# Layer 0's low half and bias on GpSimd, quarter tiles in layer 3, and a new instruction order: a four-layer graph network on one core

## The chip, the core and the metric

The kernel runs on one core of one Trainium2 chip. The core has five engines, each with its own queue of instructions that it works off in order: TensorE (PE; matrix products, with its weight loads shown as PEld), VectorE (DVE), ScalarE (ACT), GpSimd (POOL) and SyncE (SP, which only starts transfers here). They wait for each other through semaphores. The metric is the time of one execution on the device in microseconds (us); lower is better.

## What is computed

16 graphs of 1024 nodes with 256 features each go through four graph layers. Every layer takes the layer norm of x, cuts it at zero, and adds the layer's result to x.

```python
h = relu(layernorm(x)); x = x + L0(h, adj)   # and so on for L1, L2, L3
# L0: relu(h @ W_upd + (adj^T @ (h @ W_msg)) / deg + bias)
# L1: 4 heads; wh = h @ W; attention = softmax(leaky_relu(e_src[i] + e_dst[j]) where adj)
#     out = relu(attention @ wh + bias) + wh, then a layer norm per head
# L2: 4 heads; the same attention with slope 0.2; elu(attention @ wh)
# L3: 1 head of width 256; attention @ wh
```

The inputs are float32 (adj is int32), and so is the output.

## The kernel before

The kernel has a fast path, `tile_factored`, and a general one behind it (`tile_general`), which runs only when a flag says that the data does not suit the fast one; with these inputs it does not run.

The softmax is factored. The exponent of leaky_relu(s + d) is the larger of two products of a part that depends on the source and one that depends on the target. So for each block of 128 target nodes (`jb`) and each head one VectorE instruction makes a tile of masked weights, `p`: the larger of a row `r` (a source part, spread over all partitions) and a column `tt`, times the mask. It stands in `masked`, line 1083, and works on 128x1024 elements in layers 1 and 2 and on 128x256 in layer 3. PE multiplies p with the projected features and sums over the eight blocks in PSUM (`acc`): 16 products of 64 columns per p in layers 1 and 2 (line 1266, shown as 32 records), two of 257 columns per p in layer 3 (line 1420). The last column of the features is the sum that the result is divided by.

Per graph the stages are:

- `layer0`: norm (`norm_t`: statistics on VectorE at 922 and 929, the inverse root on GpSimd at 934 and 935, normalised rows `hn` on ScalarE at 954, transposes on PE at 967, copies to `ht` at 973); the projection with W_msg (984); the split of the messages into a high half `hi`, rounded to PE's faster float32r, and a low half `lo`. For `lo` PE adds minus `hi` to the projection in PSUM with a product by -I (`minus`, 1119), and ScalarE copies the rest out (1129). Then eight gathers over the adjacency (1143 with hi, 1146 with lo), the degree (1154), its inverse on GpSimd (1157, 1158), the scaled messages `o` (1164); and for each pair of blocks a product of ones with the bias, itself in two float32r halves (`pair`, `b0`, 1173), with the products of h with W_upd on top (1182). VectorE adds `o` and that (1194) and then x (1201).
- `heads` for layers 1 and 2: norm, projection (984, copied out at 1003), `terms`: the source parts are raised (`es`, 1024), turned by PE (1034), copied into a p tile (1038), written to DRAM (`rd`, 1042) and read back spread over the partitions (`r`, 1067); three reductions keep bounds of the exponents for the flag (`f_mx`, 1050 to 1052); the target parts are raised (1057, 1058) and multiplied into the features (`weigh`, 1247). Then 4 heads of 8 p each; after each head an epilogue (`epilogue1`, `epilogue2`; from 1285 on: divide, bias, norm per head with GpSimd's root at 1339 and 1340, or elu with 1381, 1382 and 1388). Three heads are added to x by a DMA that GpSimd starts (1216), the last by VectorE (1227).
- `layer3`: the same with one head; four quarters of the nodes, each with 8 p of 128x256 and two accumulators; then the inverse (1434), the result with x added (1445), and the store (1459).

The order of all this on the engines is not that of the program. Every step is put into a plan by `do`, with its engine, a cost in us, what it reads and writes, and a priority: `plan.pos` (PE work so far, moved by `SHIFT` per graph) plus a number from the table `RANK` for its stage and engine. `Plan.emit` then always issues the step that could start earliest by these costs, the lower priority first among equals. A tile of a kind is there as often as `BUFS` says (six p, two hn, two acc, three x), and a step waits in the plan until one is free. So several graphs are under way at once, and the order on each engine is fixed when the kernel is built. A graph's plan may not begin before layer 3 of the graph two before it (`gates`).

```python
self.ops.append((eng, cost, lag, fn, deps, bufs, self.pos + slack + RANK[self.stage][ENGINES.index(eng)], kind, dma))
...
if at is not None and (best is None or (at, prio, k) < best):
    best = (at, prio, k)
```

Of the kernel before, what the change touches and what calls it, by code (L numbers as in the profile page):

```python
# [8 lines left out]
F32 = mybir.dt.float32  # L9
# [9 lines left out]
P = 128  # L19
# [7 lines left out]
SHIFT = 38.75  # L27

ENGINES = ("pe", "dve", "act", "pool", "sp")
RANK = {  # L30
    "load": (-255, -45, -146, -223, -161),
    "setup": (147, 44, -129, 45, 72),
    "norm0": (132, -159, -111, 18, -3),
    "split0": (-94, 119, -51, -165, -111),
    "mask": (77, 143, 41, 193, 218),
    "gather0": (241, -7, 71, 23, 10),
    "norm1": (-60, -62, -162, -146, -99),
    "project1": (20, 26, -5, 26, -6),
    "weights1": (-164, 7, -45, 57, -13),
    "heads1": (-192, -212, -213, -62, -111),  # L40
    "last1": (-26, -102, 9, -196, -80),
    "norm2": (-206, -157, 81, 6, -21),
    "project2": (79, -60, -360, 87, -40),
    "weights2": (94, -3, 153, -153, 12),
    "heads2": (-112, -33, -288, -105, -59),
    "last2": (-21, -230, -230, -36, -82),
    "norm3": (-477, -373, -518, -355, -261),
    "project3": (148, 162, -14, -78, 0),
    "weights3": (170, 143, 167, 44, 87),
    "last3": (43, -259, -75, -14, -59),  # L50
# [4 lines left out]
    "mv": 4, "st": 2, "rstd": 4, "shift": 4, "tt": 3, "es": 2, "dg": 2, "rden": 2, "sth": 1, "mh": 2, "rsh": 2,  # L55
# [16 lines left out]
class Plan:  # L72
# [8 lines left out]
    def __init__(self):  # L81
        self.ops, self.pos, self.gate, self.stage = [], 0.0, None, None

    def do(self, eng, cost, fn, r=(), w=(), lag=0.0, slack=0.0, kind="f", dma=0.0):
# [25 lines left out]
        self.ops.append((eng, cost, lag, fn, deps, bufs, self.pos + slack + RANK[self.stage][ENGINES.index(eng)], kind, dma))  # L110
# [3 lines left out]
    def emit(self):  # L114
# [7 lines left out]
        kept, moved = "f", 0.0  # L122
# [6 lines left out]
        while ready:  # L129
            best = None  # L130
            for k in ready:
                eng, cost, lag, fn, deps, bufs, prio, kind, dma = self.ops[k]
# [18 lines left out]
                if at is not None and (best is None or (at, prio, k) < best):  # L151
                    best = (at, prio, k)
            at, _, k = best
            eng, cost, lag, fn, deps, bufs, _, kind, dma = self.ops[k]
# [444 lines left out]
def tile_factored(  # L599
# [46 lines left out]
    minus = const.tile([P, P], F32R, name="f_minus")  # L646
    nc.vector.tensor_scalar(minus, ident, -1.0, None, op0=ALU.mult)
# [8 lines left out]
    mx = const.tile([P, B * 9], F32, name="f_mx")  # L656
    rdn = const.tile([P, B * NB], F32, name="f_rdn")

    pair = const.tile([2, 1], F32R, name="f_pair")
    nc.gpsimd.memset(pair.bitcast(F32), 1.0)  # L660
# [24 lines left out]
    b0 = kept("f_bias0", [2, D], F32R)  # L685
# [139 lines left out]
    def weights():  # L825
# [3 lines left out]
        y = buf(work, "y", [P, 2 * D])  # L829
        fetch(y, "in", lambda t: t[0:1, :D], bias0.rearrange("(o d) -> o d", o=1))  # L830

        def parts():
            nc.vector.tensor_copy(b0.t[0:1, :], y.t[0:1, :D])
            nc.vector.tensor_tensor(
                y.t[0:1, D:].bitcast(F32R), y.t[0:1, :D], b0.t[0:1, :].bitcast(F32), op=ALU.subtract
            )

        do("dve", 0.7, parts, r=[(y, "in")], w=[(y, "lo"), (b0, 0)])
        do(
            "pool",  # L840
            0.8,
            lambda: nc.gpsimd.dma_start(b0.t[1:2, :], y.t[0:1, D:].bitcast(F32R)),
            r=[(y, "lo")],
            w=[(b0, 1)],
            lag=2.5,
        )
# [61 lines left out]
    def norm_t(xs, by_block=False):  # L908
# [3 lines left out]
        for hf in range(2):  # L912
# [34 lines left out]
            for i2 in range(2):  # L947
# [21 lines left out]
                do("pe", 0.46, turn, r=[hn], w=[pt])  # L969
# [8 lines left out]
    def project(ps, ht, ib, w, lo, hi, k=0):  # L978


        def go():
            out = ps.t[:, : hi - lo] if hi - lo > D else ps.t[:, k, :]
            for c in range(KC):
                nc.tensor.matmul(  # L984
                    out,
                    ht.t[:, c, ib * P : (ib + 1) * P],
                    w.t[:, c, lo:hi],
                    start=(c == 0 and k == 0),
                    stop=(c == KC - 1),
                    skip_group_check=k > 0,  # L990
                )

        do("pe", 0.88, go, r=[(ht, ib // 2), w], w=[ps])
# [15 lines left out]
    def terms(wh, nh, slope, ecol, scol, k):  # L1009


        tt = buf(small, "tt", [P, NB, nh])
        r4 = buf(work, "p", [P, N])
        rd = buf(dram, "rd", [nh, N])

        def ed():
# [3 lines left out]
        es = buf(small, "es", [P, nh, NB])  # L1020
# [4 lines left out]
                es.t, wh.t[:, :, scol : scol + nh].rearrange("p n h -> p h n"), AF.Exp, scale=1.0 - slope  # L1025
            ),
            r=[(wh, ib) for ib in range(NB)],
            w=[es],
# [5 lines left out]
            lambda: nc.tensor.transpose(pt.t[:m, :P], es.t.rearrange("p h n -> p (h n)"), ident),  # L1034
            r=[es],
# [12 lines left out]
        def bounds():  # L1048
            es = wh.t[:, :, scol : scol + nh]
            nc.vector.tensor_reduce(mx[:, k : k + 1], ed(), AX.XY, ALU.max)  # L1050
            nc.vector.tensor_reduce(mx[:, k + 1 : k + 2], ed(), AX.XY, ALU.min, negate=True)
            nc.vector.tensor_reduce(mx[:, k + 2 : k + 3], es, AX.XY, ALU.max)

        do("dve", 0.4, bounds, r=[wh])

        def raise_t():
            nc.scalar.activation(tt.t, ed(), AF.Exp, scale=-(1.0 - slope))
            nc.scalar.activation(ed(), ed(), AF.Exp)

        do("act", 0.5, raise_t, w=[tt, wh])  # L1060
# [14 lines left out]
        return tt, spread  # L1075

    def masked(r, tt, mask, jb, h, lo, hi):

        w = buf(work, "p", [P, N])
# [4 lines left out]
                w.t[:, : hi - lo], r.t[:, lo:hi], tt.t[:, jb, h : h + 1], mask.t[:, jb, lo:hi], op0=ALU.max, op1=ALU.mult  # L1084
            ),
            r=[r, tt, mask],
            w=[w],
# [4 lines left out]
    def layer0(b, xs, adjr, mask):  # L1092
# [11 lines left out]
        for n in range(0, NB, 2):  # L1104
            ps = buf(mm_p, "mm", [P, 2, D])
            for k in range(2):
# [9 lines left out]
            do(  # L1116
                "pe",
                0.23,
                lambda n=n, ps=ps: nc.tensor.matmul(
                    ps.t, minus, hi.t[:, n : n + 2, :D], start=False, stop=True, skip_group_check=True  # L1120
                ),
                r=[(hi, ib) for ib in parts],
                w=[ps],
                kind="r",
            )
# [3 lines left out]
                lambda n=n, ps=ps: nc.scalar.copy(lo.t[:, n : n + 2, :D], ps.t),  # L1129
                r=[ps],  # L1130
                w=[(lo, ib) for ib in parts],
# [4 lines left out]
        for jb in range(NB):  # L1136
# [35 lines left out]
            def update(pu=pu, j0=jb - 1):  # L1172
                nc.tensor.matmul(
                    pu.t,
                    pair.to_broadcast([2, P]),
                    b0.t.rearrange("k (o d) -> k o d", o=1).to_broadcast([2, 2, D]),
                    start=True,
                    stop=False,
                )
                for q in range(2):  # L1180
                    for c in range(KC):
# [4 lines left out]
                            start=False,  # L1186
                            stop=(q == 1 and c == KC - 1),
                        )

            do("pe", 2.17, update, r=[(ht, jb // 2), (dg, "in"), w0, b0], w=[pu], kind="rf")  # L1190
# [42 lines left out]
    def heads(b, l, xs, mask, w, slope, epilogue, keep):  # L1233
# [19 lines left out]
        for h in range(H):  # L1253
# [5 lines left out]
            for jb in range(NB):  # L1259
# [14 lines left out]
                do("pe", 0.94, product, r=[p, xw], w=[ps], kind="c")  # L1274
# [276 lines left out]
```

## Time and profile before

| | before |
|---|---|
| median of 3 runs | 2740.81 us (2739.89 to 2741.58) |
| the profiled execution | 2741.27 us, span 2739.4 us |
| PE's granted clock, mean over the span | 0.972 of full |
| masked weights, 128x1024 (L1083, VectorE) | 1024 instructions, 1251.0 us busy, mean 1276 ns |
| masked weights, 128x256 (L1083, VectorE) | 512 instructions, 222.4 us busy, mean 477 ns |
| head products (L1266, PE) | 32768 records, 1064.6 us busy; 135.7 us idle before them |
| layer 3 products (L1420, PE) | 2048 records, 462.2 us busy; 10.1 us idle before them |
| GpSimd's inverse root of the heads (L1340) | 64 instructions of 128x8, mean 2348 ns |
| row r read back (L1067, SyncE's queue) | 144 transfers, median 3.9 us from issue to landing |

The profile is of one execution, and its span is what lies between the first and the last instruction. A group of instructions is given by line, engine, operation, tiles (out<-in) and shapes, with its busy time and mean duration; behind the bar stands how long the engine was idle just before such instructions, and what ended that. Instructions of one engine overlap a little, so that busy times count a bit double: p of 128x1024 takes 1276 ns, but the next one starts 1196 ns after it. In a timeline every line has a start, a duration, the engine and the instruction, merged where several of one kind follow each other; a bracket shows the idle time before it and who ended it.

### The profile page before, as it was taken

The page shows a single profiled execution, that of the slowest core. Times are in us where ns is not written, and L with a number is a line of the kernel's source. Part 1 is how long each engine was busy: PE and PEld are TensorE (multiplying, and loading weights), DVE is VectorE, ACT ScalarE, POOL GpSimd, SP SyncE. Part 2 cuts the span into 40 slices and gives each one's busy share as a digit, 9 for nine tenths or more (in the row PEclk, how much of TensorE's full clock was granted, in tenths as well). Part 3 has the DMA queues.
Part 4 walks back from the last instruction along what each step waited for, and adds up shares of the span by engine and source line. Part 5 has one row for each costly group of instructions (what it writes and reads, how often), then busy time and mean ns, then how long its engine had stood idle before and what let it go on. Part 6 is the DMA issues. An engine that isn't in the chain of part 4 may idle for free. (4 is left out here: it accounts for less than half of the span.)

```text
span 2739.4 us, 92386 instructions
## 1 busy us (share of the span) xinstructions
PE 2547.4 (93%) x40667; PEld 2285.7 (83%) x40667; DVE 2357.3 (86%) x4790; ACT 1143.5 (42%) x2753; POOL 878.0 (32%) x907
## 2 busy tenths in 40 slices
PE   7867999999999999999999999999999999999786
PEld 6767798888888888889888889888888988888775
DVE  2699689898988989899898989989898898989884
ACT  4431625344353444525344452534435353453222
POOL 3332234324252332424224251422425133241210
PEclk9989999999999999999999999999999999999998
DMA  8724547356472745547255563735546263562121
GB/s 194 171 44 84 113 87 165 82 128 117 99 143 53 159 91 129 105 91 163 60 144 97 118 125 71 163 75 133 112 107 134 63 158 81 130 118 66 33 52 29
DMA packets 397318, 293.58 MB, mean 107 GB/s; under 512 B 179301, under 2 KB 345706, under 8 KB 396906
## 3 DMA queue, kind: packets, MB, share of 16 engines
q0 software_dynamic: 232992, 92.29, 24.8%
q1 hardware_dynamic: 160752, 193.05, 24.4%
q8 instruction: 321, 5.26, 0.8%
q10 hardware_dynamic: 3162, 2.24, 0.3%
q14 instruction: 91, 0.75, 0.1%
HBM read 228.21 MB, written 17.37 MB: 90 GB/s over the span
## 5 line engine op out<-in xcount | busy, mean ns | idle before, releaser
L1083 DVE SCALAR_TENSOR_TENSOR p<-r,tt,mask 128x1024 f32<-128x1024 f32 (+1 forms) x1536 | 1473.3, 1010 | 109.2 <-PE acc L1266 40.8
L1266 PE MATMUL acc<-wide,p 128*64 128x65 f32 x32768 | 1064.6, 227 | 135.7 <-DVE p L1083 129.3
L1266 PEld LDWEIGHTS acc<-wide,p 128*64 128x64 f32 x32768 | 1017.2, 141 | 204.0 <-issue 99.0
L984 PE MATMUL mm<-f_w,ht 128*128 128x264 f32 (+2 forms) x2048 | 477.0, 387 | 1.4 <-ACT ht L973 1.3
L1420 PE MATMUL acc<-wide,p 128*128 128x257 f32 x2048 | 462.2, 382 | 10.1 <-DVE p L1083 9.9
L1420 PEld LDWEIGHTS acc<-wide,p 128*128 128x128 f32 x2048 | 386.1, 191 | 68.1 <-issue 11.1
L984 PEld LDWEIGHTS mm<-f_w,ht 128*128 128x128 f32 x2048 | 384.6, 192 | 61.2 <-ACT ht L973 3.0
L954 ACT ACTIVATE hn<-x,shift,rstd 128x256 f32<-128x256 f32 x512 | 269.1, 591 | 257.5 <-DVE shift L941 157.1
L1356 ACT ACTIVATE t<-t,mh,rsh 128x64 f32<-128x64 f32 x512 | 176.7, 428 | 198.2 <-DVE mh L1346 174.3
L1143 PE MATMUL mm<-wide,adjr 128*128 128x258 f32 x1024 | 254.5, 289 | 0.0
L1146 PE MATMUL mm<-wide,adjr 128*128 128x256 f32 x1024 | 247.9, 282 | 0.0
L1003 ACT COPY wide<-mm 128x264 f32<-128x264 f32 (+1 forms) x384 | 141.3, 378 | 218.7 <-PE mm L984 216.5
L1216 POOL DMA_DIRECT2D x<-y x48 | 76.6, 1596 | 447.4 <-DVE y L1388 435.8
L934 POOL TENSOR_SCALAR rstd<-mv 128x4 f32<-128x4 f32 x128 | 60.7, 474 | 434.6 <-DVE mv L929 402.3
L1143 PEld LDWEIGHTS mm<-wide,adjr 128*128 128x128 f32 x1024 | 195.9, 191 | 1.7
L1146 PEld LDWEIGHTS mm<-wide,adjr 128*128 128x128 f32 x1024 | 194.2, 190 | 1.5
L922 DVE BATCH_NORM_STATS2 st<-x 128x6 f32<-128x256 f32 x512 | 183.2, 412 | 8.4 <-DMA x<-in_x_dram 5.6
L967 PE MATMUL mm<-f_ident,hn 128*128 128x128 f32 x1024 | 168.0, 300 | 20.2 <-ACT hn L954 17.2
L973 ACT COPY ht<-mm 128x512 f32<-128x512 f32 x256 | 137.8, 580 | 104.9 <-PE mm L967 103.9
L1157 POOL TENSOR_SCALAR dg<-f_deg 128x1 f32<-128x1 f32 x128 | 61.0, 476 | 359.7 <-ACT f_deg L1154 357.4
L967 PEld LDWEIGHTS mm<-f_ident,hn 128*128 128x128 f32 x1024 | 125.2, 151 | 50.4 <-ACT hn L954 35.5
L935 POOL TENSOR_TENSOR rstd<-rstd,f_mhalf 128x4 f32<-128x4 f32 x128 | 162.2, 1268 | 10.7
(103 smaller groups left out, 2179.3 us busy)
## 6 DMA issues: line engine op xcount, KB each, us to landing
r<-rd SPq DMA_DIRECT2D x144, 512.0 KB, 3.9
adjr<-in_adj_dram POOLq DMA_DIRECT2D x128, 512.0 KB, 4.7
nat<-in_adj_dram SPq DMA_DIRECT2D x128, 512.0 KB, 6.6
out_dram<-o SPq DMA_DIRECT2D x64, 256.0 KB, 2.8
x<-in_x_dram SPq DMA_DIRECT2D x31, 512.0 KB, 5.1
x<-t POOLq DMA_DIRECT2D x48, 256.0 KB, 5.5
x<-y POOLq DMA_DIRECT2D x48, 256.0 KB, 4.5
mask<-sq SPq DMA_TRANSPOSE x128, 4.7
```

Source lines behind the costliest of these rows:

```text
L922: lambda st=st, ib=ib, k=k: nc.vector.bn_stats(st.t[:, k, :], xs.t[:, ib, :]),
L935: nc.gpsimd.tensor_tensor(rstd.t, rstd.t, mhalf[:, :nh], op=ALU.pow)
L954: nc.scalar.activation(hn.t[:, k, :], xs.t[:, hf * nh + q, :], AF.Relu, bias=shift.t[:, q : q + 1], scale=rstd.t[:, q : q + 1],)
L967: nc.tensor.transpose(pt.t[:, k, c, :], hn.t[:, k, c * P : (c + 1) * P], ident)
L984: nc.tensor.matmul(out, ht.t[:, c, ib * P : (ib + 1) * P], w.t[:, c, lo:hi], start=(c == 0 and k == 0), stop=(c == KC - 1), skip_group_che ...
L1003: lambda ib=ib, ps=ps: nc.scalar.copy(wh.t[:, ib, :cols], ps.t[:, :cols]),
L1083: lambda: nc.vector.scalar_tensor_tensor(w.t[:, : hi - lo], r.t[:, lo:hi], tt.t[:, jb, h : h + 1], mask.t[:, jb, lo:hi], op0=ALU.max, op1= ...
L1143: nc.tensor.matmul(ps.t[:, : D + 2], a.t[:, ib, :], hi.t[:, ib, : D + 2], start=(ib == 0), stop=False)
L1146: nc.tensor.matmul(ps.t[:, :D], a.t[:, ib, :], lo.t[:, ib, :D], start=False, stop=(ib == NB - 1))
L1266: nc.tensor.matmul(ps.t[c : c + 64, g, q * E1 : (q + 1) * E1], p.t[:, i2 * 64 : (i2 + 1) * 64], xw.t[:, jb, h * E1 : (h + 1) * E1], start= ...
L1356: nc.scalar.activation(t.t[:, ib, :], t.t[:, ib, :], AF.Identity, bias=mb.t[:, 3, ib : ib + 1], scale=rs.t[:, ib : ib + 1],)
L1420: nc.tensor.matmul(ps.t[:, q, : D + 1], w.t[:, q * P : (q + 1) * P], wh.t[:, jb, : D + 1], start=(jb == 0), stop=(jb == NB - 1),)
```

## The change

The parts of the diff are these.

- Layer 0's low half: the product by -I is gone. ScalarE copies the whole projection from PSUM into a tile of the kind hn (`raw`), and GpSimd subtracts hi from it, 128x512 elements at a time, four times a graph.
- Layer 0's bias: the product with ones is gone, with `pair` and the split of the bias. The bias is loaded once, spread over all partitions, and GpSimd adds it to the scaled messages `o`, 128x512 at a time, four times a graph.
- Layer 3: four p of 128x256 share one p tile, a quarter each, so that six tiles hold 24.
- `terms`: the raised source and target parts lie in one tile `et`, the turned source part has a tile of its own (`r4`) instead of a p tile, and the bounds are taken after raising with two reductions instead of three, with a later priority.
- The plan: a new `RANK` and `SHIFT`, a starting number for each graph (`START`), p kept in the order of the program within a graph (`row`), p put first when none is in stock (`LOW`, `FIRST`), a hold that lets a step of lower priority number go first if it could start a little later (`HOLD`), and some costs changed. The order on every engine comes out differently.

```diff
-SHIFT = 38.75
+SHIFT = 50.0
+
+LOW, FIRST = 1, 288
 
 ENGINES = ("pe", "dve", "act", "pool", "sp")
+HOLD = (0.0, 0.25, 0.05, 0.0, 0.0)
+
+START = (428, 493, 356, 309, 254, 248, 242, 107, 64, 31, -43, -148, -235, -329, -280, -568)
 RANK = {
...
-    "gather0": (241, -7, 71, 23, 10),
+    "gather0": (-34, -156, -171, 38, -118),
...
-    "weights1": (-164, 7, -45, 57, -13),
+    "weights1": (-176, 10, 31, -19, 1),
...
-    "mv": 4, "st": 2, "rstd": 4, "shift": 4, "tt": 3, "es": 2, "dg": 2, "rden": 2, "sth": 1, "mh": 2, "rsh": 2,
+    "mv": 4, "st": 2, "rstd": 4, "shift": 4, "et": 3, "r4": 1, "dg": 2, "rden": 2, "sth": 1, "mh": 2, "rsh": 2,
...
+        if row is not None:
+            if row in self.rows:
+                deps.add(self.rows[row])
+            self.rows[row] = k
+        self.ops.append((eng, cost, lag, fn, deps, bufs, self.pos + slack + RANK[self.stage][ENGINES.index(eng)], kind, dma, stock))
...
+                if stock > 0 and store < LOW:
+                    prio -= FIRST
...
-                if at is not None and (best is None or (at, prio, k) < best):
-                    best = (at, prio, k)
-            at, _, k = best
-            eng, cost, lag, fn, deps, bufs, _, kind, dma = self.ops[k]
+                if at is not None:
+                    could.append((at, prio, k))
+                    if best is None or could[-1] < best:
+                        best = could[-1]
+            at, prio, k = best
+            until = at + HOLD[ENGINES.index(self.ops[k][0])]
+            for a, p, q in could:
+                if self.ops[q][0] == self.ops[k][0] and a <= until and p < prio:
+                    at, prio, k = a, p, q
+            eng, cost, lag, fn, deps, bufs, _, kind, dma, stock = self.ops[k]
+            store += stock
...
-    b0 = kept("f_bias0", [2, D], F32R)
+    b0 = kept("f_bias0", [P, D])
...
+        fetch(b0, "in", lambda t: t, bias0.rearrange("(o d) -> o d", o=1).to_broadcast([P, D]))
...
+        def raise_t():
+            nc.scalar.activation(et.t[:, 1], ed().rearrange("p n h -> p h n"), AF.Exp, scale=-(1.0 - slope))
+            nc.scalar.activation(ed(), ed(), AF.Exp)
+
+        do("act", 0.5, raise_t, w=[(et, 1), wh])
+
         def bounds():
-            es = wh.t[:, :, scol : scol + nh]
-            nc.vector.tensor_reduce(mx[:, k : k + 1], ed(), AX.XY, ALU.max)
-            nc.vector.tensor_reduce(mx[:, k + 1 : k + 2], ed(), AX.XY, ALU.min, negate=True)
-            nc.vector.tensor_reduce(mx[:, k + 2 : k + 3], es, AX.XY, ALU.max)
-
-        do("dve", 0.4, bounds, r=[wh])
-
-        def raise_t():
-            nc.scalar.activation(tt.t, ed(), AF.Exp, scale=-(1.0 - slope))
-            nc.scalar.activation(ed(), ed(), AF.Exp)
-
-        do("act", 0.5, raise_t, w=[tt, wh])
+            nc.vector.tensor_reduce(mx[:, k : k + 2], et.t.rearrange("p s h n -> p s (h n)"), AX.X, ALU.max)
+            nc.vector.tensor_reduce(mx[:, k + 2 : k + 3], ed(), AX.XY, ALU.max)
+
+        do("dve", 0.45, bounds, r=[et, wh], slack=24.857)
...
+    def masked(r, tt, mask, jb, h, lo, hi, w=None, q=0):
+
+
+        w = w or buf(work, "p", [P, N])
+        c = q * (hi - lo)
         do(
             "dve",
             (hi - lo + 125) / 960.0,
             lambda: nc.vector.scalar_tensor_tensor(
-                w.t[:, : hi - lo], r.t[:, lo:hi], tt.t[:, jb, h : h + 1], mask.t[:, jb, lo:hi], op0=ALU.max, op1=ALU.mult
+                w.t[:, c : c + hi - lo],
+                r.t[:, lo:hi],
+                tt.t[:, 1, h, jb : jb + 1],
+                mask.t[:, jb, lo:hi],
+                op0=ALU.max,
+                op1=ALU.mult,
             ),
-            r=[r, tt, mask],
-            w=[w],
+            r=[r, (tt, 1), mask],
+            w=[(w, q)],
+            row="weights",
+            stock=1,
...
-            do(
-                "pe",
-                0.23,
-                lambda n=n, ps=ps: nc.tensor.matmul(
-                    ps.t, minus, hi.t[:, n : n + 2, :D], start=False, stop=True, skip_group_check=True
-                ),
-                r=[(hi, ib) for ib in parts],
-                w=[ps],
-                kind="r",
-            )
+            raw = buf(work, "hn", [P, 2, D])
             do(
                 "act",
                 0.48,
-                lambda n=n, ps=ps: nc.scalar.copy(lo.t[:, n : n + 2, :D], ps.t),
+                lambda raw=raw, ps=ps: nc.scalar.copy(raw.t, ps.t),
                 r=[ps],
+                w=[raw],
+            )
+            do(
+                "pool",
+                1.3,
+                lambda n=n, raw=raw: nc.gpsimd.tensor_tensor(
+                    lo.t[:, n : n + 2, :D],
+                    raw.t,
+                    hi.t[:, n : n + 2, :D].bitcast(F32),
+                    op=ALU.subtract,
+                ),
+                r=[raw, *((hi, ib) for ib in parts)],
                 w=[(lo, ib) for ib in parts],
...
             def update(pu=pu, j0=jb - 1):
-                nc.tensor.matmul(
-                    pu.t,
-                    pair.to_broadcast([2, P]),
-                    b0.t.rearrange("k (o d) -> k o d", o=1).to_broadcast([2, 2, D]),
-                    start=True,
-                    stop=False,
-                )
                 for q in range(2):
                     for c in range(KC):
                         nc.tensor.matmul(
                             pu.t[:, q, :],
                             ht.t[:, c, (j0 + q) * P : (j0 + q + 1) * P],
                             w0.t[:, c, D:],
-                            start=False,
-                            stop=(q == 1 and c == KC - 1),
+                            start=(q == 0 and c == 0),
+                            stop=(c == KC - 1),
+                            skip_group_check=q > 0,
                         )
 
-            do("pe", 2.17, update, r=[(ht, jb // 2), (dg, "in"), w0, b0], w=[pu], kind="rf")
+            do("pe", 1.78, update, r=[(ht, jb // 2), (dg, "in"), w0], w=[pu])
+            do(
+                "pool",
+                1.3,
+                lambda o=o: nc.gpsimd.tensor_tensor(
+                    o.t, o.t, b0.t.rearrange("p (o d) -> p o d", o=1).to_broadcast([P, 2, D]), op=ALU.add
+                ),
+                r=[b0],
+                w=[o],
+            )
...
-                w = masked(r, tt, mask, jb, 0, i2 * 2 * P, (i2 + 1) * 2 * P)
-
-                def product(w=w, ps=ps, jb=jb):
-                    for q in range(2):
+                q = jb % 4
+                w = masked(r, tt, mask, jb, 0, i2 * 2 * P, (i2 + 1) * 2 * P, w if q else None, q)
+
+                def product(w=w, ps=ps, jb=jb, q=q):
+                    for k in range(2):
+                        c = (2 * q + k) * P
                         nc.tensor.matmul(
-                            ps.t[:, q, : D + 1],
-                            w.t[:, q * P : (q + 1) * P],
+                            ps.t[:, k, : D + 1],
+                            w.t[:, c : c + P],
                             wh.t[:, jb, : D + 1],
                             start=(jb == 0),
                             stop=(jb == NB - 1),
                         )
 
-                do("pe", 0.87, product, r=[w, (wh, jb)], w=[ps])
+                do("pe", 0.875, product, r=[(w, q), (wh, jb)], w=[ps], stock=-1)
...
+        plan.rows = {}
+        plan.pos, plan.gate = b * SHIFT + START[b], gates.get(b)
         xs, adjr = load_x(b) if b else first, {k: load_adjr(b, k) for k in range(2)}
```

## The prediction

> **What bounds the kernel now.** I read the page's first lines, then the list of waits, the groups by shape, and the timeline of one graph's boundary.
>
> ```profile
> PE 2547.4 (93%) x40667; PEld 2285.7 (83%) x40667; DVE 2357.3 (86%) x4790; ACT 1143.5 (42%) x2753; POOL 878.0 (32%) x907
> ```
> ```profile
> PE acc L1266 <- DVE p L1083: 129.3, 56, 8.5
> DVE f_mx L1050 <- ACT wide L1003: 111.1, 21, 11.5
> ```
> TensorE (PE) and VectorE are both nearly full, and what PE waits for is almost only the masked weights p of VectorE. So the time is set by how the two fit together, not by PE's load alone. From about 426 us on the trace repeats every 162.1 us, a graph each. One boundary, read from the timeline (start, duration):
>
> ```profile
> 1375.83 4.07 PE L1266 MATMUL acc<-wide,p 128*64 128x65 f32 x133
> ...
> 1382.20 0.21 DVE L1285 RECIPROCAL rden<-acc 128x8 f32<-128x8 f32 x1 [0.65 <-PE acc L1266]
> 1382.21 5.37 PE L1420 MATMUL acc<-wide,p 128*128 128x257 f32 x24
> 1382.44 0.69 DVE L1286 TENSOR_TENSOR t<-acc,rden 128x512 f32<-128x512 f32 x1
> ...
> 1384.63 0.68 DVE L1388 SCALAR_TENSOR_TENSOR y<-y,t 128x512 f32<-128x512 f32 x1
> 1385.35 0.69 DVE L1227 TENSOR_TENSOR x<-x,y 128x512 f32<-128x512 f32 x1
> ...
> 1389.24 0.14 DVE L1434 RECIPROCAL f_rdn<-acc 128x2 f32<-128x2 f32 x1
> 1389.41 0.88 DVE L1445 SCALAR_TENSOR_TENSOR o<-acc,f_rdn,x 128x256 f32<-128x256 f32 x2
> ...
> 1390.28 2.47 DVE L1083 SCALAR_TENSOR_TENSOR p<-r,tt,mask 128x1024 f32<-128x1024 f32 x2
> ...
> 1391.70 2.00 PE L1266 MATMUL acc<-wide,p 128*64 128x65 f32 x32 [4.12 <-DVE p L1083]
> ```
> The last head of layer 2 ends at 1382.2. VectorE then finishes that head, adds it to x and takes the statistics of the next norm: all in order, until 1389.2. Then it writes out the last quarter of layer 3, and only then makes the first p of the next layer 1. PE has 5.4 us of layer 3 to cover this and stands for 4.12. This stall comes 15 times; with a smaller one of 0.55 it is 4.7 us a graph.
>
> **PE work removed.** I work with start-to-start times in the trace, since busy times overlap. The bias product delays what follows by 0.43 us, the minus product by 0.31; each comes 64 times: 27 + 20 = 47 us, or 3.0 a graph. The busy times below (31.6 + 24.2 = 55.8) are the upper end.
>
> ```profile
> L1173 PE MATMUL mm<-f_bias,f_pair 2*128 2x512 f32 x64 | 31.6, 494 | 0.0
> L1119 PE MATMUL mm<-wide,f_minus 128*128 128x512 f32 x64 | 24.2, 451 | 0.7 <-ACT wide L1112 0.7
> ```
> With the other products (64 head products at 0.93, 32 of layer 3 at 0.87, 32 projections at 0.89, 16 update products at 0.44, 128 gathers at 0.12, 64 transposes at 0.11) a graph has 148.5 us of PE's own work now and 145.5 after. VectorE's own work is 145.0 in both, its starts counted the same way: three reductions become two, which saves some 0.1 us each.
>
> **ScalarE** copies as often as before, into a work tile (hn's two buffers) instead of lo. A norm behind it may wait for GpSimd's read, a microsecond at most; ScalarE is 42% busy, and I take nothing.
>
> **GpSimd's 128 new 128x512 operations** (64 subtractions, 64 bias additions). No row shows one. The Trainium skill (GPSIMD Engine Reference, section 3.1) has 4.5 us for 2048 elements, so I estimate 1.1 to 1.3 us each: 150 us more on an engine that is busy for 878. Behind each in its queue wait the head roots and the DMAs of adjr and of x; the gather waits for the fourth subtraction. In the new order 7 us of head products lie between the projections and that gather, so this is covered; without cover it costs 2 us a graph.
>
> What matters is the port. The rows:
>
> ```profile
> 593.28 1.25 DVE L1083 SCALAR_TENSOR_TENSOR p<-r,tt,mask 128x1024 f32<-128x1024 f32 x1
> 593.54 1.09 POOL L934 TENSOR_SCALAR rstd<-mv 128x4 f32<-128x4 f32 x1 [10.79 <-DVE mv L929]
> ...
> 596.29 0.23 POOL L934 TENSOR_SCALAR rstd<-mv 128x4 f32<-128x4 f32 x1 [0.54 <-ACT wide L1003]
> ...
> 605.61 3.67 DVE L1083 SCALAR_TENSOR_TENSOR p<-r,tt,mask 128x1024 f32<-128x1024 f32 x3
> ...
> 607.03 2.55 POOL L1340 TENSOR_TENSOR rsh<-rsh,f_mhalf 128x8 f32<-128x8 f32 x1
> ```
> L934 takes 0.23 us alone, and 1.09 when it must wait for the end of VectorE's p. So GpSimd does wait for p. The other way round nothing is seen: three p take 3.67 us although L1340 runs in their midst; in 48 of 48 such cases the next p starts 1.20 us after the one before. The Trainium skill (SBUF — State Buffer, "Who interferes with whom") says of a VectorE instruction with two SBUF inputs and a GpSimd one that reads SBUF that whoever is second "fully blocks" for the whole instruction. By the rule the additions cost VectorE up to 1.2 us each, by the row nothing. But the row's operands have 8 elements, the new ones 512. Bounds: 0 to 150 us of VectorE time; no gain is possible, since nothing leaves VectorE. I take the row for the forecast and the rule for a rival.
>
> **Quarter tiles** let VectorE be 24 layer 3 steps ahead where it was 6, with no instruction more.
>
> **The new order**, from the lists of instructions of both kernels. After a graph's last product of layer 3 come 32 gathers (3.8 us), and three head p are made before the last quarter is written out: the 4.12 us stall goes, and with it the 0.55. But the transpose that the next layer 1's weights need, and behind it the first head product, now stand directly behind layer 2's last head, with nothing of layer 3 between. By the rows above VectorE needs 1389.24 - 1382.20 = 7.04 us for head, x and statistics, then 1.2 for p: PE stands 8.3 us there. The DMA chain beside it is shorter: r is issued 2.0 us after the transpose and lands 3.9 later, p follows. So the stall moves and grows. Sum per graph: -3.0 - 4.7 + 8.3 = +0.6; 162.7.
>
> The check from VectorE's side: in the new order VectorE sets the pace from the boundary until some 100 us later, and the largest lag of a p behind its product, by both sums, is 9.4 us, against 3.5 now; waits of VectorE itself add 4 to 6 in either. It gives 161 to 163. So the middle is a wash, and this stretch has no slack for GpSimd's port.
>
> **The ends.** Before: 426 us to the end of graph 0's layer 3, 13 graphs of 162.1, and 206. In the new order PE has 252 us of own work up to that point instead of 309. VectorE's run there stays 167 us of own work (170 now, which took 188): 105 to the first p, 185, then 74 of PE: 364. The next graph has little lag: 159. Then 11 of 162.7 = 1790. What follows has 332 us of PE's and 339 of VectorE's work, and VectorE sets the first 261 of it, then 104 of PE alone; with waits of 30 (now 12% of VectorE's time): 395. Sum 364 + 159 + 1790 + 395 = 2708, set against the profiled execution (2741.3; span 2739.4, 2 around it). The median of the runs is 2740.8, half a microsecond off. So -33 us, of which the ends give nearly all.
>
> **Rivals.**
> *The port blocks VectorE (slower).* Four subtractions and one or two bias additions of each graph fall into VectorE's unslack stretch, where over three quarters of the work (p above all) has two SBUF inputs: 5 x 1.0 = 5 us a graph, 12 graphs, 60 us: 2768. For: L934's wait, the rule, 512 elements. Against: the 48 undelayed p. It decides from 0.55 us per addition, where 12 x 5 x 0.55 eats the 33 us.
> *The new stall doesn't bite.* If waits elsewhere make the 8.3 us overlap and PE is bound by its work, the removed work (47) and the old stall (15 x 4.7 = 70) both go: 2624. Against: the order is fixed, and the product needs p.
> *A wash.* What PE saves, VectorE-bound stretches give back, and the start saves less than the tail loses: 2740.
>
> **Chances.** Forecast, 2685 to 2735: 0.45; better than that, with part of the second rival: 0.17; a wash, within 0.2% (about what a measurement of this kernel tells from no change): 0.08; slower by the port: 0.30. Range 2650 to 2785: from half of the second rival to the first with a little more delay per addition.
>
> **What would show it.** Right: L1119's and L1173's groups gone; a wait of about 8 us of PE for p once a graph, at layer 1's first head, and none behind layer 3; a period near 163; the first layer 3 ending near 364 us; p at 1.28 us as now. Wrong: p's mean or its gaps grown by 0.5 us or more around GpSimd's additions (the port); a period below 158 (the stall is covered); or the gather waiting for lo.

## The result, and the profile after

The changed kernel takes 2813.7 us (median of 4 runs, 2812.3 to 2816.6) against 2740.4 for the kernel before: the ratio is 1.027, 95% interval 1.0255 to 1.0291. It is slower, where 2708 was forecast. The profiled execution has a span of 2812.2 us. Its first line of busy times, and the longest wait of TensorE (us in total, times, longest):

```profile
PE 2504.4 (89%) x40539; PEld 2262.0 (80%) x40539; DVE 2448.3 (87%) x4739; ACT 1144.7 (41%) x2753; POOL 1056.1 (38%) x1039
```
```profile
PE acc L1281 <- DVE p L1085: 202.2, 124, 8.1
```

TensorE is busy for 43 us less than before, VectorE for 91 us more, although the change gives it no new work. TensorE's waits for p have grown from 129 to 202 us. Some groups by shape (busy time, mean ns of one, then the idle time before):

```profile
L1085 DVE SCALAR_TENSOR_TENSOR p<-r,et,mask 128x1024 f32<-128x1024 f32 x1024 | 1320.3, 1341 | 52.0 <-DMA r<-rd 25.4 <-PE acc L1281 22.1 <-PE acc L1437 3.3
L1136 POOL TENSOR_TENSOR wide<-hn,wide 128x512 fp32r<-128x512 f32 x64 | 104.7, 1651 | 34.9 <-ACT hn L1129 34.9
L1200 POOL TENSOR_TENSOR o<-o,f_bias 128x512 f32<-128x512 f32 x64 | 99.6, 1557 | 16.4 <-ACT o L1176 16.3
L1361 DVE SCALAR_TENSOR_TENSOR mh<-mh,rsh 128x8 f32<-128x8 f32 x64 | 27.3, 427 | 1.8 <-POOL rsh L1355 1.8
```

The mean p took 1276 ns before and takes 1341. That mean hides two kinds. In the trace 120 of the 1024 wide p lie beside one of GpSimd's additions; 64 of those take about 2.3 us (63 of them 2.29 to 2.36), and the other 56 and all the rest 1.28. An instruction of 128x8 (L1361, 165 ns before) can be held for as long: 16 of its 64 take 1.02 to 1.26 us. One p that is held, in VectorE's timeline and in GpSimd's:

```profile
1155.33 7.08 DVE L1085 SCALAR_TENSOR_TENSOR p<-r,et,mask 128x1024 f32<-128x1024 f32 x5
```
```profile
1155.84 1.90 POOL L1200 TENSOR_TENSOR o<-o,f_bias 128x512 f32<-128x512 f32 x1
```

The addition is issued while the first p runs, and waits for it to end (it takes 1.26 us alone, 1.90 here). Then the second p waits for the addition. The five p take 7.08 us; where the additions are cut away (below), the same five take 6.06.

The new stall is where the prediction put it, and as long. The boundary in the timeline:

```profile
1088.18 3.95 PE L1281 MATMUL acc<-wide,p 128*64 128x65 f32 x128
...
1092.06 0.28 PE L1036 MATMUL mm<-f_ident,et 128*32 128x128 f32 x1
...
1095.20 0.69 DVE L1242 TENSOR_TENSOR x<-x,y 128x512 f32<-128x512 f32 x1
...
1099.09 1.25 DVE L1085 SCALAR_TENSOR_TENSOR p<-r,et,mask 128x1024 f32<-128x1024 f32 x1
...
1100.40 3.74 PE L1281 MATMUL acc<-wide,p 128*64 128x65 f32 x64 [8.05 <-DVE p L1085]
```

TensorE ends layer 2's last head, turns the sources, and stands for 8.05 us until VectorE has finished that head, added it to x, taken the statistics (1095.9 to 1099.1) and made the first p.

The span cut at the ends of the layer 3 products, beside the forecast's terms and three experiments that are told below (us):

| | forecast | after | additions cut away | bias cut away | products put back |
|---|---|---|---|---|---|
| to graph 0's layer 3 | 364 | 367.2 | 364.0 | 364.9 | 366.9 |
| next graph | 159 | 173.4 | 170.4 | 170.5 | 173.0 |
| 11 graphs, each | 162.7 | 168.17 | 165.50 | 165.63 | 166.55 |
| the rest | 395 | 421.7 | 418.9 | 416.6 | 420.1 |
| span | 2708 | 2812.2 | 2773.8 | 2773.9 | 2792.1 |

### The profile page after: what moved, and what is told of

Same layout as the page of the kernel before. It is cut to its first block, busy times and chain, and to the rows that moved or that the text cites. A ratio compares the mean times of both kernels' runs of the same rounds, so it can differ in the third digit from the quotient of the medians.

```text
span 2812.2 us, 92071 instructions
## 1 busy us (share of the span) xinstructions
PE 2504.4 (89%) x40539; PEld 2262.0 (80%) x40539; DVE 2448.3 (87%) x4739; ACT 1144.7 (41%) x2753; POOL 1056.1 (38%) x1039
## 5 line engine op out<-in xcount | busy, mean ns | idle before, releaser
L1085 DVE SCALAR_TENSOR_TENSOR p<-r,et,mask 128x1024 f32<-128x1024 f32 (+1 forms) x1536 | 1534.9, 1054 | 71.7 <-DMA r<-rd 36.7
L1281 PE MATMUL acc<-wide,p 128*64 128x65 f32 x32768 | 1078.0, 227 | 239.2 <-DVE p L1085 202.2
L970 PE MATMUL mm<-f_ident,hn 128*128 128x128 f32 x1024 | 161.9, 290 | 39.8 <-ACT hn L957 33.0
L970 PEld LDWEIGHTS mm<-f_ident,hn 128*128 128x128 f32 x1024 | 116.6, 145 | 69.1 <-ACT hn L957 50.9
```

The costliest lines, as they stand in the source:

```text
L970: nc.tensor.transpose(pt.t[:, k, c, :], hn.t[:, k, c * P : (c + 1) * P], ident)
L1085: lambda: nc.vector.scalar_tensor_tensor(w.t[:, c : c + hi - lo], r.t[:, lo:hi], tt.t[:, 1, h, jb : jb + 1], mask.t[:, jb, lo:hi], op0=ALU ...
L1281: nc.tensor.matmul(ps.t[c : c + 64, g, q * E1 : (q + 1) * E1], p.t[:, i2 * 64 : (i2 + 1) * 64], xw.t[:, jb, h * E1 : (h + 1) * E1], start= ...
```

## Experiments

Every ratio is against the kernel before on the same chip. The theories: A, GpSimd's additions hold VectorE up; B, the new order is at fault.

### How much of it is GpSimd

All in the new kernel's own order. In `e1_tiny_both` (and for its half in `e2_tiny_sub` and `e3_tiny_bias`):

```diff
-                lambda raw=raw, ps=ps: nc.scalar.copy(raw.t, ps.t),
+                lambda n=n, ps=ps: nc.scalar.copy(lo.t[:, n : n + 2, :D], ps.t),
...
-                    lo.t[:, n : n + 2, :D],
-                    raw.t,
-                    hi.t[:, n : n + 2, :D].bitcast(F32),
+                    lo.t[:, n : n + 2, :1],
+                    lo.t[:, n : n + 2, :1].bitcast(F32),
+                    hi.t[:, n : n + 2, :1].bitcast(F32),
...
-                    o.t, o.t, b0.t.rearrange("p (o d) -> p o d", o=1).to_broadcast([P, 2, D]), op=ALU.add
+                    o.t[:, :, :1], o.t[:, :, :1], b0.t[:, :1].rearrange("p (o d) -> p o d", o=1).to_broadcast([P, 2, 1]), op=ALU.add
```

> The changed kernel in its own order on every queue, with GpSimd's 128 additions cut from 512 columns to 2 (ScalarE writes the low half's tile, and GpSimd subtracts in one column of each block only; the bias is added to one column of each block only: most of the subtraction and of the bias is left out). Theory A (the additions hold up VectorE's weights p): p back from 1.34 to about 1.28 us in the mean, period of a graph from 168 to about 163 us, time near 2710 us (2690 to 2730). Theory B (the new order is at fault: the 8 us stall and the long tail; GpSimd is hidden): no more than 20 us come back, 2790 or more.

Measured: 2773.2 us, ratio 1.0117 (1.0097 to 1.0137). No p is held any more (126 lie beside a cut addition), and their mean is 1278 ns. But only 40 us come back, and the kernel is still slower than before. Both theories missed: A by about 60 us, B by about 20.

> As e1_tiny_both, but only the subtraction is cut to one column of each block; the bias is added in full. Theory A: a part of the gain of e1_tiny_both, about half (2745 to 2785 us), and the two parts add up to it. Theory B: 2790 or more. If one of the two additions lies where VectorE sets the pace and the other where it has slack, this kernel and the next lie far apart.

Measured: 2812.6 us, 1.0258 (1.0239 to 1.0276). Cutting the subtraction is worth 1 us.

> The changed kernel with only the bias addition cut to one column of each block; the subtraction is whole. Theory A: the other half, 2745 to 2785 us. Theory B: 2790 or more.

Measured: 2776.5 us, 1.0138 (1.0121 to 1.0155). Cutting the bias is worth 37 us. Yet the subtraction holds VectorE longer: with it alone 39 wide p are held, with the bias alone 16. The group of L1301 (the division of a head, on VectorE) shows why; first with both additions cut, then with the subtraction in place:

```profile
L1301 DVE TENSOR_TENSOR t<-acc,rden 128x512 f32<-128x512 f32 x128 | 88.5, 692 | 52.2 <-DMA x<-t 48.0 <-DVE rden L1300 0.2
```
```profile
L1301 DVE TENSOR_TENSOR t<-acc,rden 128x512 f32<-128x512 f32 x128 | 88.5, 692 | 4.6 <-DVE rden L1300 0.2
```

Once a graph VectorE has to wait 4.0 us for a transfer that still reads the t tile. That is 59 us behind the start of the 8 us stall. The subtractions come at 44 to 52 us and hold VectorE for 4.2 us a graph: they take up that wait, and the period stays (165.50 and 165.63). The bias additions come at 64 to 128 us, behind it. They hold VectorE for 3.3 us a graph (3.0 without the subtractions), little takes that up, and the period grows by 2.5 to 2.9. So the same lock is free at one place and costs nearly its full length at another. (A rival, that VectorE waits for the sum `o` itself, is small: 10.6 us in the whole trace, 8.2 of them in its first 109 us.)

`e9_one_input` makes the bias addition an operation with one operand from SBUF:

```diff
-                lambda o=o: nc.gpsimd.tensor_tensor(
-                    o.t, o.t, b0.t.rearrange("p (o d) -> p o d", o=1).to_broadcast([P, 2, D]), op=ALU.add
-                ),
+                lambda o=o: nc.gpsimd.tensor_scalar(o.t, o.t, b0.t[:, :1], None, op0=ALU.add),
```

> The changed kernel, with GpSimd's bias addition made a tensor-with-scalar operation over the same 128x512 tile: one operand from SBUF instead of two (it adds the bias's first value to all columns; all are zero). Subtraction unchanged. If only a GpSimd operation with two operands holds VectorE up, the time falls to that of e3_tiny_bias, about 2776 us, and p beside it stays at 1.28 us. If any long GpSimd operation does, it stays at 2805 to 2815.

Measured: 2794.6 us, 1.0197 (1.0179 to 1.0214): between the two. The same five p and the addition, in VectorE's and GpSimd's timelines:

```profile
1150.20 6.49 DVE L1085 SCALAR_TENSOR_TENSOR p<-r,et,mask 128x1024 f32<-128x1024 f32 x5
```
```profile
1150.74 2.20 POOL L1200 TENSOR_SCALAR o<-o,f_bias 128x512 f32<-128x512 f32 x1
```

6.49 us for five: the p behind this addition takes 1.71 us instead of 2.30. It is held for 0.43 us instead of 1.03, although the operation itself is longer (1.58 us alone against 1.26). Neither expectation had a part of the lock.

### How much of it is the order

`e4_order_alone` keeps the new order, the quarter tiles and the new `terms`, and puts both products back, in place of the additions:

```diff
-            raw = buf(work, "hn", [P, 2, D])
...
+            def rest(n=n, ps=ps):
+                nc.tensor.matmul(ps.t, minus, hi.t[:, n : n + 2, :D], start=False, stop=True, skip_group_check=True)
+                nc.scalar.copy(lo.t[:, n : n + 2, :D], ps.t)
...
+                nc.tensor.matmul(
+                    pu.t,
+                    pair.to_broadcast([2, P]),
+                    b0.t.rearrange("k (o d) -> k o d", o=1).to_broadcast([2, 2, D]),
+                    start=True,
+                    stop=False,
+                )
```

> The new order and the quarter tiles with the products put back on TensorE at the places of the copies and updates, and no addition on GpSimd (the low half of the bias, which is zero, is left out). TensorE has 47 us more work than in the changed kernel. Theory A: about 2745 us (2730 to 2765): the 47 us come back on TensorE, the contention goes. Theory B: 2813 + 47 = about 2860 us, at the least 2820.

Measured: 2793.6 us, 1.0196 (1.0177 to 1.0214), between A and B. Two things follow. With TensorE's work the same as before, the new order with its tiles and `terms` costs 53 us. And the 47 us of products are worth only 20 us of time (2793.6 - 2773.2): 1.05 us a graph (166.55 - 165.50), not 3.0.

`e5_gpsimd_alone` is the reverse: the order before, with GpSimd in place of the products. `e8_sub_alone` does it for the subtraction only. In both ScalarE's copy goes to one tile of 128x512 (there is no room for two):

```diff
+            def rest(n=n, ps=ps):
+                raw = work.tile([P, 2, D], F32, name="f_raw", bufs=1)
+                nc.scalar.copy(raw, ps.t)
+                nc.gpsimd.tensor_tensor(
+                    lo.t[:, n : n + 2, :D], raw, hi.t[:, n : n + 2, :D].bitcast(F32), op=ALU.subtract
+                )
```

> The kernel before, its order kept on every queue, with only the products replaced: the 64 products with the negated identity and the 64 bias products are gone from TensorE, GpSimd subtracts (after ScalarE's copy) and adds the bias (the first 64 values of the bias, repeated; all are zero). TensorE has 47 us less work. Theory A (the bias addition costs some 40 us through VectorE, the subtraction nothing, in any order): the saving of TensorE, 20 to 47 us (20 is what it was worth in the new order), less 40: 2733 to 2760 us. Theory C (the port's cost is a matter of where the additions lie, and only the new order puts them on VectorE's limiting stretch): 2695 to 2720 us.

> The kernel before in its own order with only the subtraction moved to GpSimd; the bias stays a product (the first 64 values of the bias, repeated; all are zero). TensorE has 64 x 0.24 = 15 us less work. If the subtraction is as free here as in the changed kernel: 2725 to 2735 us. If the port charges it here: 2745 or more.

Measured: 2872.0 us, 1.047 (1.0452 to 1.0487), and 2826.9 us, 1.0306 (1.0289 to 1.0323). No expectation came near. The waits of e5:

```profile
PE mm L1144 <- POOL wide L1120: 70.1, 29, 3.2
ACT f_raw L1119 <- POOL wide L1120: 67.2, 32, 3.4
```

In the old order the gather stands close behind the projections, and waits for GpSimd's low half, 4.9 us a graph in the steady part. In e8 this wait is 4.8 of the 5.7 us by which a graph is longer; in e5, where a graph is 8.8 us longer, it leaves other waits that were not taken apart. Part of it is the single raw tile: ScalarE waits for it too. So these two runs say that the exchange needs an order that puts work ahead of the gather, as the new one does; they do not price the lock in the old order.

`e6_quarter_alone` is the kernel before with quarter tiles and its own planner:

> The kernel before with layer 3's weights in quarters of one tile, and nothing else of the change (its planner moves what follows from it). Theory: the 4.2 us stall behind layer 3, once a graph, came from the six tiles that layer 3's narrow weights used up; with quarters VectorE runs ahead and most of 14 x 4.2 = 59 us comes back: 2685 to 2715 us. Rival: the stall has another cause (VectorE's order), and only its place changes: 2730 or more.

Measured: 2928.6 us, 1.0693 (1.0664 to 1.0722). With the old table of priorities the planner made a quite different order, so it tells nothing of the tiles. `e10_quarter_old_order` plans with single tiles, keeps that order, and lets four steps share one real tile:

```diff
+            own = w.make
+
+            def shared():
+                if not four:
+                    four.append(own())
+                return four[0]
+
+            w.make = shared
```

> The kernel before, its order kept on every queue, with layer 3's weights in quarters of one tile and nothing else. VectorE's 35 us of waits for layer 3's products to give a tile back go. Theory D (the stall behind layer 3 stands in VectorE's queue, as the prediction read it: head, x, statistics, the last quarter's output, then p): the 4.2 us stall stays, 2725 to 2742 us. Rival (the six narrow tiles cause it): 2680 to 2710 us. e6_quarter_alone was slower through its other order, so it said nothing on this.

Measured: 2766.8 us, 1.0100 (1.0081 to 1.0118). The stall behind layer 3 stays, at 4.29 us, as theory D has it; but the kernel is 25 us slower, which neither had. VectorE's waits for products to release a tile, before and in e10:

```profile
DVE p L1083 <- PE acc L1266: 40.8, 29, 3.0
```
```profile
DVE p L1093 <- PE acc L1276: 83.2, 43, 4.8
```

The wide p wait longer for a tile: 42 us more, while the 35 us of waits in layer 3 are gone. That fits a shared tile, which is free only when its last quarter is used; no run tried it apart.

### What a stall is worth

The prediction added and subtracted stalls of TensorE. `e7b_early_head` shortens the new one; `e11_p_before_output` and `e12_p_before_norm` shorten the old one. All three move only p (e7b also the transposition that r comes from). In e11 and e12, as a list of VectorE's queue (+ where p stands now, - where it stood):

```
 x<-x,y
+p, p (e12)
 st, mv, st, mv
+p, p (e11)
 f_rdn, o, o (layer 3's last output)
 shift
-p, p
 shift
```

> The changed kernel, where in the repeating graphs the transposition that starts layer 1's r rows stands ahead of three of the four products it was queued behind (2.9 us), and VectorE's first two weights p of layer 1 stand ahead of the next layer's statistics (3.2 us). If the 8.0 us stall is the chain transposition to r rows to first p: it falls to about 5 us and the time by some 11 x 2.9 = 32 us, to about 2780. If the stretch behind the stall is paced by VectorE's p anyway (1.28 us each against 0.94 us of products), the stall is only moved: 2800 to 2815 us.

> The kernel before, with one thing moved on VectorE's queue: the first two weights p of the next layer 1 stand ahead of the output of layer 3's last quarter (1.05 us in the timeline), once a graph. If a stall of TensorE is worth its length (the prediction's bookkeeping: 4.7 us a graph for the old stall): 14 x 1.05 = 15 us, 2726 us. If VectorE's whole queue sets the pace and the stall only shows where it is late: no gain, 2735 to 2745.

> As e11_p_before_output, but the two p stand ahead of the norm's statistics too (3.3 us more), directly behind the addition to x. Bookkeeping by stalls: the 4.1 us stall is gone, 14 x 4.1 = 57 us, 2684 us. If VectorE's queue sets the pace: the stall comes back a few products later or behind the late norm, 2735 to 2775, as e7b_early_head gave for the new order.

Measured: e7b 2844.8 us, 1.037 (1.0352 to 1.0387), which is 31 slower than the changed kernel; e11 2759.0, 1.0072 (1.0058 to 1.0085); e12 2791.1, 1.0185 (1.0172 to 1.0199). Not "no gain" but a loss, the larger the further p goes ahead. TensorE's waits of before, e11 and e12 in turn:

```profile
PE mm L967 <- ACT hn L954: 17.2, 15, 7.8
```
```profile
PE acc L1294 <- DVE p L1109: 114.0, 55, 8.5
PE mm L993 <- ACT hn L980: 38.8, 29, 7.8
```
```profile
PE acc L1294 <- DVE p L1109: 102.0, 56, 8.5
PE mm L993 <- ACT hn L980: 87.6, 28, 7.8
```

In e11 the wait for p falls as counted, from 129.3 to 114.0 (15 us). In e12 it falls to 102.0, by 27 us where 57 were counted: VectorE now comes to p before the row r has landed, and stands there itself. Its waits for r, before and in e12:

```profile
DVE p L1083 <- DMA r<-rd: 17.6, 4, 11.0
```
```profile
DVE p L1109 <- DMA r<-rd: 52.2, 21, 10.8
```

In both, p stands ahead of the norm's statistics or its shift now, and the transpositions of the normalised rows (L993), which stand a few products behind on TensorE, wait for those: 17.2 becomes 38.8 and 87.6. VectorE serves two customers at the boundary, and the move robs one for the other. The granted clock goes down as well (mean of the profiled run 0.972 before, 0.966 in e11, 0.964 in e12): in the repeating part of e11 TensorE is busy for 157.4 us a graph with the products that took 156.6, which is 0.8 of the 1.3 us by which a graph is longer.

What remained open was whether a stall is worth its length when nothing else is made late. `e13_output_later` and `e14_output_one_later` shorten the same stall by putting only layer 3's output (1.05 us) later, in the same list:

```
 st, mv, st, mv
-f_rdn, o, o
 shift
 p, p
+f_rdn, o, o (e14)
 shift
+f_rdn, o, o (e13)
```

The list is that of the traces. In e14 the output stands behind both p, where the expectation has it behind the first only; so the second p comes sooner too, and just the second shift keeps its place.

> The kernel before, with only the output of layer 3's last quarter (the reciprocal and two products on VectorE, 1.05 us) put later on VectorE's queue: behind the first two p of the next layer 1 and the second shift of the norm. Nothing that TensorE waits for is put later: the first shift, both p and the second shift come 1.05 us sooner. If a stall is worth its length as long as no other customer of VectorE is made late: 14 x 1.05 = 15 us, 2725 us (2720 to 2732). If the stall's length says nothing even then: 2735 to 2745.

> As e13_output_later, but the output goes behind the first p only, so the second p and the second shift keep their place. First theory: the first p and the first shift come 1.05 us sooner, TensorE's products after the first and the second transposition wait as before: part of the gain, 2725 to 2738. Second theory: 2735 to 2745.

Measured: e13 2729.9 us, 0.9956 (0.9942 to 0.9969); e14 2722.6 us, 0.9933 (0.992 to 0.9946), 18 us faster than the kernel before and the fastest of all kernels here. The waits of e14, and one of VectorE's in e13:

```profile
PE acc L1297 <- DVE p L1112: 113.9, 54, 8.5
PE mm L996 <- ACT hn L983: 16.9, 15, 7.8
```
```profile
DVE shift L970 <- POOL rstd L964: 18.1, 18, 2.0
```

In both the wait for p is down by 15 us, as in e11, and the transpositions wait no longer than before. 14 x 1.05 = 15 us were counted, 11 and 18 measured. In e13 VectorE pays: its second shift comes too early and stands 0.94 us a graph for GpSimd's root (18.1 us in all, 4.9 before and in e14). In the repeating part of e14 TensorE waits 1.0 us a graph less for p, the length of what was moved, and is busy for 0.6 less with the same products (156.0 instead of 156.6; mean granted clock 0.977 instead of 0.972). Together that is the 1.6 us by which the graph is shorter. So a stall was worth its length where nobody else paid, and a little more with the higher clock.

## Why the prediction was wrong, step by step

Two terms of the sum per graph failed: GpSimd's additions, put at nothing, and the removed products, put at their full length. Outside the repeating graphs, the next graph and the rest were put too short as well.

- **What bounds the kernel** was read rightly: PE waits for p, and how the two engines fit sets the time.
- **The start** came out, and so did its first part: the first p at 102.0 us where 105 was counted, and the end at 367.2 for 364 (364.0 without the additions). (The mark of 426 us for before was read ten us late; the trace has 416.1. The rest behind it is then 216, and the sum holds.)
- **The port failed.** "I take the row for the forecast and the rule for a rival": the row was an operation on 8 elements, the change brings 512, and the rival's price of 1.0 us per held p was right (1.03). The rival's 60 us were 40 (2813.7 - 2773.2); its "four subtractions and one or two bias additions" named the wrong ones as well: the subtractions are taken up by a wait of VectorE, and nearly all the cost is the bias. The 2768 of that rival was still too low, since the other terms failed too.
- **PE work removed, "3.0 a graph"**: mis-sized. Its length was right, its worth was 1.05 a graph, measured in the new order. TensorE's waits for p, with the products (e4) and without them (e1):

```profile
PE acc L1285 <- DVE p L1091: 133.0, 49, 8.1
```
```profile
PE acc L1281 <- DVE p L1085: 172.4, 77, 8.3
```

In the repeating part TensorE is busy for 3.2 us a graph less without the products, but waits 3.0 more for p (8.05 and 11.04); other waits shrink by 0.9. VectorE does not come sooner because TensorE has less to do.
- **The stalls, "-4.7" and "+8.3"**: nearly right. The new stall is 8.05 us, none is left behind layer 3 (the old one came 14 times, not 15), and the order with its tiles cost 166.55 - 162.1 = 4.4 a graph where 3.6 was counted. Waits for p make up 3.3 of that (4.7 us a graph before, 8.05 in e4); the rest was not taken apart. The granted clock, 0.972 before and 0.963 in e4, is not the cause: TensorE is busy for 156.6 us a graph in both.
- **The sum per graph**: 162.1 + 4.4 (order) - 1.05 (products) + 2.7 (additions, 168.17 - 165.50) = 168.2. These terms are differences between kernels, so that they must add up; what they show is where the forecast's +3.6, -3.0 and 0 were off. That is 5.5 us a graph, 60 us in 11.
- **The check from VectorE's side** ("waits of VectorE itself add 4 to 6 in either") did not hold: in the repeating part VectorE's idle gaps add up to 15.8 us a graph before, 14.2 after, and 19.1 without the additions. With its busy time they give the period. The middle of the span in after and in e1 (length, then each engine's busy time):

```profile
529.00:2379.00 1850.00, 1698.11 (x27844) 1542.36 (x27843) 1693.45 (x3238) 787.78 (x1896) 739.50 (x704) 0.97 0.57 108
```
```profile
523.00:2343.00 1820.00, 1686.43 (x27841) 1545.42 (x27840) 1610.36 (x3238) 786.80 (x1895) 679.87 (x704) 0.97 0.61 110
```

The third busy time is VectorE's: 83 us more in 11 graphs, 7.6 each. Its gaps shrink by 4.9, so that 2.7 remain.
- **The next graph, "has little lag: 159"**: 173.4, and 170.4 without the additions. The new order's stalls are there from the first graph on.
- **The rest, 395**: 421.7, of which the additions are 3. The waits allowed for were too few; which of them come from the order was not taken apart.
- **Quarter tiles, "with no instruction more"**: true, but in the old order they cost 25 us, with longer waits for a tile. How the 4.4 us a graph divide between tiles and order in the new one stays open: the new order needs the 24 places, and no run has it without them.
- **ScalarE, and the gather waiting for lo**: nothing of weight in the new order, where TensorE waits for lo 0.8 us in all; in the old one the missing cover cost PE 70 us of waits (e5), above the "2 us a graph" that the prediction gave.

The parts, then: 40 of the 106 us between forecast and result are the port, and 65 are the order with its tiles and removed products that were worth less than their length. Without the additions (e1) the 65 fall on the 11 repeating graphs (31), the next graph (11) and the rest (24).

## What to carry to other kernels

Work moved off a nearly full engine is worth less than its length when another engine is as full, and here it went to the one engine that locks that other out: price a GpSimd operation by a row of its own size, and by where it falls, since a wait of VectorE just behind it can make it free. A stall is a fair unit of account only if the cure makes nobody else late: look for the instruction that no one waits for soon (here layer 3's output) and move that, not the one that is waited for; and see that what comes up in its place is ready by then (in e13 the shift was not). A change of several parts with a new order should be split before it is judged: each part that could be tried alone was slower.

## What the runs showed of the hardware

The runs show a lock in both directions between a VectorE instruction with two operands in SBUF, as p has, and a GpSimd instruction that reads SBUF. GpSimd waits for VectorE: the addition beside p took 1.90 us instead of 1.26. VectorE waits for GpSimd: a 128x512 addition with two operands, 1.26 us long when nothing holds it, holds p for 1.03 us, and the one-operand form, 1.58 us long, for only 0.43. GpSimd's root on 128x8, 1.65 us at its shortest and 2.35 in the mean, holds none of 97 p beside it in the kernel before. So in these forms the duration of a GpSimd instruction in the profile is no measure of how long it locks; the elements and operands that it reads come nearer. VectorE's statistics, with one input from SBUF, were not held: they took 414 ns beside an addition (18 of them) and 411 elsewhere.

The Trainium skill (SBUF — State Buffer, "SBUF: two separate sides") says that a VectorE instruction with two SBUF inputs and a GpSimd one that reads SBUF take a shared pair of ports in turn, and that whichever starts first keeps it for the whole instruction while the other blocks. The traces agree on the lock. On its length they differ: 0.43 us of the 1.58 that the one-operand form takes in the profile.
